# A chain of four layers on one core: the first batch in plain fp32, with filler products on TensorE between its steps

## The chip, the cores and the metric

The program runs on one core of a Trainium2 chip. The metric is the time of one execution in microseconds (us), the median of several runs. The engines are TensorE (PE in the profile, its weight loads PEld), VectorE (DVE), ScalarE (ACT), GpSimd (POOL) and SyncE (SP), whose queue issues most of the DMA transfers. Each engine works through its own list of instructions in order.

## The reference

Sixteen batches of a 256 x 256 matrix pass through four layers, each added to its input. Cut to what matters:

```python
# layer 0, per batch; ema(b, tau): h = alpha * h + b along the sequence
ctx = ema(x, tau_ctx)
gated = x * sigmoid(concat(x, ctx) @ Wg.T + bg)
mod = 0.5 + sigmoid(gelu(x @ Wn1.T + bn1) @ Wn2.T + bn2)      # 16 columns, one per decay
temporal = sum_d blend_w[d] * ema(gated * mod[..., d], tau[d])  # 16 decays
gate = sigmoid(temporal @ Wtemp.T + btemp)
soma = gelu(x @ Wsoma.T + bsoma)
x = x + layernorm((soma * gate) @ Wout.T) * gamma + beta
# layer 1: masked softmax over the sequence
scores = tanh(x @ W1 + b1) @ v
x = x + softmax(where(mask[type_b], scores, -1e30)) @ x / count
# layer 2: 8 experts and a shared one, all used by every batch (gates as factors)
x = x + sum_e c[b, e] * (silu(x @ Wg[e]) * (x @ Wu[e])) @ Wd[e]   # 9 experts of 256 x 1024
# layer 3: gelu MLP whose last 64 output columns use an expert chosen per batch
x = x + concat(h @ W2 + b2, h @ We[idx_b] + be[idx_b]),  h = gelu(x @ W1 + b1)
```

## The kernel before

*Products.* fp32 data are split into a high part that is rounded to fp32r, and a low part, the rest: `rnd` (L88 and L90) makes the first, `low` (L95) the second. `mm3` (L101 to L103) then makes three fp32r products in the place of one: high by high, high by low, low by high.

*Small weights.* Those of layers 0 and 1 (N1, G, SO, TE, OU, W1 for Wn1, Wg, Wsoma, Wtemp, Wout and layer 1's W1) are loaded by `load_small` (L127) into tiles that belong to other work and split by `split_small` into wh and wl.

*Layers 0 and 1.* Two generators hand them out in steps: `traces(b)` (21 steps, or 13 for batch 0) up to temporal, `pooled(b)` (10 steps) for the rest. Names to follow in the trace: ph, hg, hs are the hidden layer of mod; pm, md, ms its output; pg and ga the gate; pb and mod the factor of one decay, bt the scan's input, tr its output, ta their sum, t its copy; pso and sm the soma. Then pt and g (gate), s, po (Wout), st, mv, rs (layernorm), x1, ptr (transpose), u and x1T, pa, th, ths (tanh), psc (scores), sc (softmax), ppt and q (transpose), pp, acc. Batch 0 (`fast`) has forms of its own: its 16 decays' sums are made on TensorE by a product with the identity (L344), its factors come from TensorE and ScalarE instead of by a transfer (mdd to mod), and its products go to two PSUM banks.

*Layers 2 and 3.* Expert weights come in 72 chunks of 384 KB, which `load_chunk` loads into one of two raw tiles and splits into one of ten ring tiles (L88, then L95 on VectorE or GpSimd). A unit (`l2_unit`) is the work of two chunks for one batch (256 columns), or of one chunk for a pair of batches (512 columns). Batch 0 rides alone for five experts, that is 20 units; then batch 1 boards and the two go on together; batches 2 and 3 board at expert pass 9 and so on. The second time a split chunk is seen, it is stored and then read back already split.

*Order.* The planner hands out steps of later batches between units; `FRONT` is the number of steps of batch 1's `traces` that are given out together with batch 0's `pooled`. A scheduler then fixes the list of each engine from priorities, with `issue_after` as an extra order for it. PSUM and SBUF tiles rotate in pools, so a tile waits for the last reader of the one before.

## Time and profile before

| what | value |
|---|---|
| runs | 2854.42, 2855.34, 2858.27 us, median 2855.34 |
| the profiled execution's own time | 2854.52 us |
| its span, first to last instruction | 2852.3 us |
| busy: TensorE, VectorE, GpSimd, ScalarE | 2781.6, 1442.2, 1295.4, 1239.2 us |
| mean granted TensorE clock | 0.993 |
| bytes moved | 371.24 MB |

The span leaves out 2.2 us around the instructions. The busy time of TensorE counts a product from its issue to a modelled end, so products that follow each other overlap, and a full TensorE is not one at its peak: what it does is read from how far the starts lie apart. In the rows below, the first number is the start or the stretch, and what stands in brackets is the idle time before an instruction and what ended it. Names are those of the tiles; `out<-in` gives them with partitions x elements.

### The profile page before, as it was taken

Reading aid. Unit: us, or ns where it says so; the run is one execution under the profiler, and the core shown is the slowest. Engines: PE = TensorE matmul, PEld = TensorE weight load, DVE = VectorE, ACT = ScalarE, POOL = GpSimd, SP = SyncE. Lnnn points to the kernel's source line nnn. Section 1 sums busy time; section 2 is a strip of 40 time slices with the busy share of each in tenths; the row PEclk is TensorE's granted clock in tenths of the full one; section 3 lists DMA queues with packets and bytes.
Section 4 is the critical chain, followed back from the end, with each engine's and each line's share of the span. In section 5 each row is a group of like instructions: output and inputs, shape, how many; then the busy total and the mean of one; then the engine's idle time right before and its main releaser. Section 6 shows DMA issues by size and latency. Waiting matters only on the chain. (4 is left out here: it accounts for less than half of the span.)

```text
span 2852.3 us, 36958 instructions
## 1 busy us (share of the span) xinstructions
PE 2781.6 (98%) x13632; PEld 2339.8 (82%) x13632; DVE 1442.2 (51%) x2661; ACT 1239.2 (43%) x2054; POOL 1295.4 (45%) x984
## 2 busy tenths in 40 slices
PE   6889889999999999999999999999999999999999
PEld 4887778888888888888888888888888888888887
DVE  7978866665665454444544445444444542222222
ACT  5565544456444533435334443344433453233433
POOL 4755544544645453543534445344454443333333
PEclk8999999999999999999999999999999999999999
DMA  3444546547443532323433143332523242222552
GB/s 106 132 144 137 162 149 217 176 144 244 149 159 120 172 123 100 118 80 92 173 105 125 40 167 117 107 118 66 181 100 110 93 159 98 89 89 76 189 196 86
DMA packets 114694, 371.24 MB, mean 130 GB/s; under 512 B 12642, under 2 KB 30930, under 8 KB 114514
## 3 DMA queue, kind: packets, MB, share of 16 engines
q1 hardware_dynamic: 113650, 368.74, 39.0%
q8 instruction: 108, 1.77, 0.3%
q14 instruction: 72, 0.59, 0.1%
q10 hardware_dynamic: 864, 0.14, 0.0%
HBM read 304.62 MB, written 64.21 MB: 129 GB/s over the span
## 5 line engine op out<-in xcount | busy, mean ns | idle before, releaser
L95 POOL TENSOR_TENSOR hh<-h,hh 128x512 fp32r<-128x512 f32 x640 | 848.4, 1326 | 1327.1 <-ACT hh L88 1307.4
L608 DVE TENSOR_TENSOR h<-h,pu 128x512 f32<-128x512 f32 x576 | 393.9, 684 | 939.6 <-PE pu L103 818.1
L88 ACT ACTIVATE hh<-h 128x512 fp32r<-128x512 f32 x640 | 403.5, 631 | 932.6 <-DVE h L608 912.4
L101 PE MATMUL pg<-x,w_e 128*128 128x512 f32 (+1 forms) x1232 | 467.3, 379 | 12.7 <-ACT x L88 5.4
L607 ACT ACTIVATE h<-pg 128x512 f32<-128x512 f32 x576 | 342.9, 595 | 306.6 <-PE pg L103 228.5
L101 PE MATMUL pu<-x,w_e 128*128 128x512 f32 (+1 forms) x1232 | 465.4, 378 | 6.5 <-ACT h L607 3.7
L103 PE MATMUL pg<-x,w_e 128*128 128x512 f32 (+1 forms) x1232 | 465.7, 378 | 4.2 <-DVE w_e L95 3.4
L102 PE MATMUL y<-hh,w_e 128*128 128x512 f32 (+1 forms) x1232 | 464.4, 377 | 3.2 <-POOL hh L95 3.2
L102 PE MATMUL pg<-x,w_e 128*128 128x512 f32 (+1 forms) x1232 | 465.3, 378 | 0.0
L103 PE MATMUL pu<-x,w_e 128*128 128x512 f32 (+1 forms) x1232 | 463.8, 376 | 0.0
L102 PE MATMUL pu<-x,w_e 128*128 128x512 f32 (+1 forms) x1232 | 463.6, 376 | 0.0
L103 PE MATMUL y<-hh,w_e 128*128 128x512 f32 (+1 forms) x1232 | 463.5, 377 | 0.0
L101 PE MATMUL y<-hh,w_e 128*128 128x512 f32 (+1 forms) x1232 | 415.6, 377 | 1.0 <-DVE acc L655 0.8
L367 POOL TENSOR_TENSOR ta<-ta,tr 128x512 f32<-128x512 f32 x225 | 308.4, 1371 | 67.6 <-DVE tr L363 53.9
L363 DVE TENSOR_TENSOR_SCAN tr<-decay,bt 128x256 f32<-128x256 f32 x450 | 285.1, 672 | 0.0
L101 PEld LDWEIGHTS pg<-x,w_e 128*128 128x128 f32 x1232 | 232.5, 189 | 56.4 <-ACT w_e L88 6.4
L101 PEld LDWEIGHTS pu<-x,w_e 128*128 128x128 f32 x1232 | 232.1, 188 | 50.5 <-ACT h L607 5.8
L103 PEld LDWEIGHTS pg<-x,w_e 128*128 128x128 f32 x1232 | 232.7, 189 | 47.8 <-DVE w_e L95 5.2
L102 PEld LDWEIGHTS y<-hh,w_e 128*128 128x128 f32 x1232 | 233.0, 189 | 47.0 <-POOL hh L95 5.5
L101 PEld LDWEIGHTS y<-hh,w_e 128*128 128x128 f32 x1232 | 231.5, 189 | 44.8 <-ACT hh L88 1.3
L103 PEld LDWEIGHTS y<-hh,w_e 128*128 128x128 f32 x1232 | 233.0, 189 | 41.7
L103 PEld LDWEIGHTS pu<-x,w_e 128*128 128x128 f32 x1232 | 232.3, 189 | 41.9
(294 smaller groups left out, 3267.5 us busy)
## 6 DMA issues: line engine op xcount, KB each, us to landing
w_e<-keep_e SPq DMA_DIRECT2D x216, 768.0 KB, 4.4
raw_e<-in_wexp_dram SPq DMA_DIRECT2D x144, 384.0 KB, 4.5
keep_e<-w_e SPq DMA_DIRECT2D x72, 768.0 KB, 4.2
mod<-mdd SPq DMA_DIRECT2D x120, 256.0 KB, 3.5
w_f<-keep_f SPq DMA_DIRECT2D x56, 384.0 KB, 3.6
raw_c<-in_comb_dram SPq DMA_DIRECT2D x32, 260.0 KB, 2.8
xr<-in_xT_dram SPq DMA_DIRECT2D x16, 256.0 KB, 3.1
xt<-in_x_dram SPq DMA_DIRECT2D x16, 256.0 KB, 2.7
```

What stands on the lines that cost most here:

```text
L88: last_of["ca"] = A.activation(out_, in_, AF.Copy)
L95: i = (V if e == "v" else G).tensor_tensor(out_, in_, h.bitcast(F32), ALU.subtract)
L101: PE.matmul(o, wh, xh, start=start, stop=False, **kw)
L102: PE.matmul(o, wh, xl, start=False, stop=False, **kw)
L103: last_of["pe"] = PE.matmul(o, wl, xh, start=False, stop=stop, **kw)
L363: V.tensor_tensor_scan(tr[:, c], decay[:, d : d + 1].to_broadcast([P, S]), bt[:, c], 0.0, ALU.mult, ALU.add)
L367: G.tensor_tensor(tacc, tacc, tr, ALU.add)
L607: A.activation(h, ps_g, AF.Silu)
L608: last_of["h"] = V.tensor_tensor(h, h, ps_u, ALU.mult)
```

## The change

Batch 0 gets two generators of its own, `first_traces` and `first_pooled`, and `traces` and `pooled` keep only the form of the others. In them every product but that of ms with sel (pb) is one fp32 product instead of three fp32r products, taken straight from the raw weights (`small`) and from unsplit data; only ms and the input of the experts (x2) are still split. The raw small weights stay in two tiles of the pools xs and accp. Their splits, which the other batches need, are handed to ScalarE and GpSimd: N1 and G behind batch 0's `first_traces`, SO, TE, OU and W1 with four decays of batch 1 (the scheduler may place them earlier). `warm(n)` puts out n fp32 products of the identity with itself, 128 columns each, into a PSUM tile that nobody reads: 10 at the start and 5, 7, 2 and 10 behind the products pt, po, pa and psc. Constants that batch 0's first steps don't need come later (`later_constants`, `coefs`), the loads of pti, sgt and gat go from ScalarE's DMA queue to SyncE's, sm of batch 0 lies in PSUM, and batch 1 gets 3 steps in place of 4 beside batch 0 (`FRONT0`).

```diff
+FRONT0 = 3
...
-    small = {}
-
-    def load_small(c0, c1, tag):
-        raw = l0.tile([P, 512], F32, tag=tag, name=f"raw_{c0}", bufs=L0_BUFS.get(tag, 1))
-        nc.sync.dma_start(raw[:, : c1 - c0], wsmall[:, c0:c1])
-        small[c0] = raw[:, : c1 - c0]
-
-    def split_small(c0, e):
-        raw = small.pop(c0)
-        c1 = c0 + raw.shape[1]
-        rnd("a", wh[:, c0:c1], raw)
-        low(e, wl[:, c0:c1], raw, wh[:, c0:c1])
+
+    raw_a = xs.tile([P, 2048], F32, tag="x2", name="small_a")
+    raw_b = accp.tile([P, 1024], F32, tag="acc", name="small_b")
+
+    def small(off, n):
+        if O_TE <= off < O_W1:
+            return raw_b[:, off - O_TE : off - O_TE + n]
+        c = off if off < O_TE else off - O_W1 + O_TE
+        return raw_a[:, c : c + n]
+
+    def load_small(c0, c1):
+        nc.sync.dma_start(small(c0, c1 - c0), wsmall[:, c0:c1])
+
+    def split_small(c0, n, e):
+        rnd("a", wh[:, c0 : c0 + n], small(c0, n))
+        low(e, wl[:, c0 : c0 + n], small(c0, n), wh[:, c0 : c0 + n])
...
-    load_small(O_N1, O_N1 + 256, "bt")
+    load_small(O_N1, O_N1 + 256)
     bl = const([P, 2, ND], F32, "bl", blend)
-    load_small(O_G, O_G + 512, "tr")
     vec = const([P, V_COLS], F32, "vec", vecs)
-    pti = const([P, NB], I32, "pti", ptype.partition_broadcast(P))
-    sgt = const([P, NB], F32, "sgt", sgate.partition_broadcast(P))
-    gat = const([P, NB, NE], F32, "gat", gates.partition_broadcast(P))
-    load_small(O_G + 512, O_G + 1024, "tr")
-    load_small(O_SO, O_SO + 512, "xo")
-    load_small(O_TE, O_TE + 512, "sc")
-    load_small(O_OU, O_OU + 512, "x1")
-    load_small(O_W1, O_W1 + 256, "mb")
+    load_small(O_G, O_G + 512)
+    load_small(O_G + 512, O_G + 1024)
+    pti = const([P, NB], I32, "pti", ptype.partition_broadcast(P), nc.sync)
+    load_small(O_SO, O_SO + 512)
+    load_small(O_TE, O_TE + 512)
+    load_small(O_OU, O_OU + 512)
+    load_small(O_W1, O_W1 + 256)
     xt_tiles = {0: load_xt(0)}
     gam = const([P, S], F32, "gam", gamma.partition_broadcast(P), nc.sync)
     bet = const([P, S], F32, "bet", beta.partition_broadcast(P), nc.sync)
     eix = const([1, NB], I32, "eix", eidx, nc.sync)
+    sgt = const([P, NB], F32, "sgt", sgate.partition_broadcast(P), nc.sync)
+    gat = const([P, NB, NE], F32, "gat", gates.partition_broadcast(P), nc.sync)
...
+    def later_constants():
...
+    def coefs():
+
+        V.tensor_copy(coef[:, :, NE], sgt)
+        V.tensor_scalar(sgt, sgt, -1.0, 1.0, ALU.mult, ALU.add)
+        V.tensor_tensor(coef[:, :, 0:NE], gat, sgt.unsqueeze(2).to_broadcast([P, NB, NE]), ALU.mult)
...
+    rest = {1: (O_SO, 512), 6: (O_TE, 512), 9: (O_OU, 512), 12: (O_W1, 256)}
+
+    def traces(b):
...
-        if fast:
-            split_small(O_N1, "v")
...
-        if fast:
-            with tc.issue_after(last_of["cx"].ins):
-                split_small(O_G, "v")
-                split_small(O_G + 512, "v")
-
-                V.tensor_copy(coef[:, :, NE], sgt)
-                V.tensor_scalar(sgt, sgt, -1.0, 1.0, ALU.mult, ALU.add)
-                V.tensor_tensor(coef[:, :, 0:NE], gat, sgt.unsqueeze(2).to_broadcast([P, NB, NE]), ALU.mult)
...
+            if b == 1 and d in rest:
+                split_small(*rest[d], "g")
...
+    def two(name):
+
+        return [ps_gu.tile([P, 512], F32, tag="gu", name=f"{name}{t}")[:, :S] for t in "gu"]
+
+    def evict(c, o, i):
+
+        if c == 0:
+            last_of["ca"] = A.activation(o, i, AF.Copy)
+        else:
+            last_of["cv"] = V.tensor_copy(o, i)
+
+    idle = ps_y.tile([P, 512], F32, tag="y1", name="idle")
+
+    def warm(n, after=None):
+
+        with tc.issue_after(after.ins) if after is not None else nullcontext():
+            for _ in range(n):
+                PE.matmul(idle[:, :P], ident, ident, start=True, stop=True)
+
+    def first_traces():
+        xr = xin_tiles.pop(0)
+        warm(10)
+        cx = ft("ta", "ctx0")
+        for c in range(2):
+            last_of["cx"] = V.tensor_tensor_scan(
+                cx[:, c], decay[:, ND : ND + 1].to_broadcast([P, S]), xr[:, c], 0.0, ALU.mult, ALU.add
+            )
+        yield
+        ph = ps_l.tile([P, 512], F32, tag="ps", name="ph0")
+        for k in range(2):
+            PE.matmul(ph[:, :S], small(O_N1 + k * P, P), xr[:, k], start=k == 0, stop=k == 1)
+        hg = l0.tile([P, S], F32, tag="hg", name="hg0")
+        A.activation(hg, ph[:, :S], AF.Gelu, bias=vec[:, V_BN1 : V_BN1 + 1])
+        pg = two("pg0")
+
+        def gates_of(ks):
+            for m in range(2):
+                for k in ks:
+                    i = xr[:, k] if k < 2 else cx[:, k - 2]
+                    PE.matmul(pg[m], small(O_G + k * S + m * P, P), i, start=k == 0, stop=k == 3)
+
+        gates_of((0, 1))
+        yield
+        pm = ps_l.tile([P, 512], F32, tag="ps", name="pm0")
+        last_of["pm"] = PE.matmul(pm[:48, :S], vec[0:64, V_WN2 : V_WN2 + 48], hg[0:64], start=True, stop=True)
+        md = l0.tile([48, S], F32, tag="md", name="md0")
+        A.activation(md, pm[:48, :S], AF.Tanh, bias=hb[:48, V_BN2 : V_BN2 + 1], scale=0.5)
+        V.tensor_scalar(md, md, 0.5, 1.0, ALU.mult, ALU.add)
+        ms = l0.tile([48, S], F32R, tag="ths", name="ms0")
+        rnd("v", ms, md)
+        low("v", ms[32:], md[32:], ms[32:])
+        yield
+        ga = ft("ga", "ga0")
+        with tc.issue_after(last_of["pm"].ins):
+            gates_of((2, 3))
+        for m in range(2):
+            A.activation(ga[:, m], pg[m], AF.Tanh, bias=hb[:, V_BG + m : V_BG + m + 1], scale=0.5)
+        for c in range(2):
+            V.scalar_tensor_tensor(ga[:, c], ga[:, c], 1.0, xr[:, c], ALU.add, ALU.mult)
+        yield
+        sm = ps_a.tile([P, 2, S], F32, tag="ga", name="sm0")
+
+        tacc = ps_y.tile([P, 2, S], F32, tag="y0", name="ta0")
+        for d in range(ND):
+            if d % 2 == 0:
+                pb = ps_gu.tile([P, 2, S], F32, tag="gu", name=f"pb0_{d}")
+                for i in range(2):
+                    last_of["pb"] = PE.matmul(
+                        pb[:, i], sel[:, d + i : d + i + 1].to_broadcast([48, P]), ms, start=True, stop=True
+                    )
+            mod = l0.tile([P, 2, S], F32, tag="mod", name=f"mod0_{d}", bufs=2)
+            for c in range(2):
+                last_of["a"] = A.activation(mod[:, c], pb[:, d % 2], AF.Copy, scale=bl[:, c, d : d + 1])
+            bt = ft("bt", f"bt0_{d}", 3)
+            e = "g" if d else "v"
+            last_of[e] = (V if e == "v" else G).tensor_tensor(bt, ga, mod, ALU.mult)
+            tr = ft("tr", f"tr0_{d}", 3)
+            for c in range(2):
+                last_of["tr"] = V.tensor_tensor_scan(
+                    tr[:, c], decay[:, d : d + 1].to_broadcast([P, S]), bt[:, c], 0.0, ALU.mult, ALU.add
+                )
+            PE.matmul(tacc, ident, tr, start=d == 0, stop=d == ND - 1)
+            if d == 5:
+                pso = ps_l.tile([P, 2, S], F32, tag="ps", name="pso0")
+                with tc.issue_after(last_of["pb"].ins):
+                    for m in range(2):
+                        for k in range(2):
+                            w = small(O_SO + k * S + m * P, P)
+                            PE.matmul(pso[:, m], w, xr[:, k], start=k == 0, stop=k == 1)
+                for m in range(2):
+                    A.activation(sm[:, m], pso[:, m], AF.Gelu, bias=vec[:, V_BSO + m : V_BSO + m + 1])
+            if d % 2:
+                yield
+        t = ft("bt", "t0", 3)
+        for c in range(2):
+            evict(c, t[:, c], tacc[:, c])
+        xt = xt_tiles.pop(0)
+        with tc.issue_after(last_of["g"].ins):
+            last_of["g"] = G.tensor_tensor(xt, xt, bet.unsqueeze(1).to_broadcast([P, 2, S]), ALU.add)
+        held[0] = xt, sm, t
+        yield
+
+    def first_pooled():
+        xt, sm, tt = held.pop(0)
+        mb = l0.tile([P, 2, S], F32, tag="mb", name="mb0")
+        kreg = nc.sync.value_load(kind_i[0:1, 0:1], min_val=0, max_val=2)
+        nc.sync.dma_start(mb, masks[bass.ds(kreg, 1)].rearrange("o p c s -> (o p) c s"))
+        pt = two("pt0")
+        sg = ft("g2", "g20")
+        for m in range(2):
+            for k in range(2):
+                i = PE.matmul(pt[m], small(O_TE + k * S + m * P, P), tt[:, k], start=k == 0, stop=k == 1)
+        warm(5, i)
+        for m in range(2):
+            last_of["ca"] = A.activation(sg[:, m], pt[m], AF.Tanh, bias=hb[:, V_BTE + m : V_BTE + m + 1], scale=0.5)
+        yield
+        for c in range(2):
+            last_of["cv"] = V.scalar_tensor_tensor(sg[:, c], sg[:, c], 1.0, sm[:, c], ALU.add, ALU.mult)
+        yield
+
+        po = two("po0")
+        st = l0.tile([P, 2, 6], F32, tag="st", name="st0")
+        mv = l0.tile([P, 2, 2], F32, tag="mv", name="mv0")
+        rs = l0.tile([P, 2], F32, tag="rs", name="rs0")
+        for k in range(2):
+            for t in range(2):
+                w = small(O_OU + k * S, S)
+                i = PE.matmul(po[t], sg[:, k, t * P : (t + 1) * P], w, start=k == 0, stop=k == 1)
+        warm(7, i)
+        x1 = ft("x1", "x10")
+        for t in range(2):
+            V.bn_stats(st[:, t], po[t])
+            V.bn_aggr(mv[:, t], st[:, t])
+        V.tensor_scalar(rs, mv[:, :, 1], 4e-5, None, ALU.add)
+        G.tensor_tensor(rs, rs, mhalf, ALU.pow)
+        for t in range(2):
+            V.scalar_tensor_tensor(po[t], po[t], mv[:, t, 0:1], gam, ALU.subtract, ALU.mult)
+        yield
+        for t in range(2):
+            last_of["cv"] = V.scalar_tensor_tensor(
+                x1[:, t], po[t], rs[:, t : t + 1], xt[:, t], ALU.mult, ALU.add
+            )
+        yield
+
+        ptr = two("ptr0")
+        for c in range(2):
+            for t in range(2):
+                PE.transpose(ptr[c][:, t * P : (t + 1) * P], x1[:, t, c * P : (c + 1) * P], ident)
+        x1T = ft("xo", "x1T0")
+        for c in range(2):
+            evict(c, x1T[:, c], ptr[c])
+        yield
+        pa = ps_l.tile([P, 512], F32, tag="ps", name="pa0")
+        for k in range(2):
+            i = PE.matmul(pa[:, :S], small(O_W1 + k * P, P), x1T[:, k], start=k == 0, stop=k == 1)
+        warm(2, i)
+        ta = l0.tile([P, S], F32, tag="th", name="th0")
+        last_of["ca"] = A.activation(ta, pa[:, :S], AF.Tanh, bias=vec[:, V_B1 : V_B1 + 1])
+        yield
+        psc = ps_l.tile([P, 512], F32, tag="ps", name="psc0")
+        i = PE.matmul(psc[:, :S], vec[0:64, V_V : V_V + 1].to_broadcast([64, P]), ta[0:64], start=True, stop=True)
+        warm(10, i)
+
+        sc = ft("sc", "sc0")
+        mx = l0.tile([P, 2], F32, tag="mx", name="mx0")
+        sums = l0.tile([P, 2], F32, tag="sums", name="sums0")
+        for j in range(2):
+            V.tensor_tensor_reduce(
+                sc[:, j], psc[:, :S], mb[:, j], -1.0, 3e38, ALU.add, ALU.min, mx[:, j : j + 1]
+            )
+            last_of["ca"] = A.activation(
+                sc[:, j], sc[:, j], AF.Exp, bias=mx[:, j : j + 1], scale=-1.0, accum_out=sums[:, j : j + 1]
+            )
+        yield
+        for j in range(2):
+            js = slice(j, j + 1)
+            V.tensor_tensor(sums[:, js], sums[:, js], cntb[:, 0, js], ALU.mult)
+            V.reciprocal(sums[:, js], sums[:, js])
+            last_of["cv"] = V.tensor_scalar(sc[:, j], sc[:, j], sums[:, js], None, ALU.mult)
+        yield
+        ppt = two("ppt0")
+        for l in range(2):
+            for j in range(2):
+                PE.transpose(ppt[l][:, j * P : (j + 1) * P], sc[:, j, l * P : (l + 1) * P], ident)
+        q = ft("bt", "q0", 3)
+        for l in range(2):
+            evict(l, q[:, l], ppt[l])
+        yield
+        pp = two("pp0")
+        for l in range(2):
+            for m in range(2):
+                PE.matmul(pp[m], x1[:, l, m * P : (m + 1) * P], q[:, l], start=l == 0, stop=l == 1)
+        for m in range(2):
+            V.tensor_tensor(acc_of(0)[:, m], x1T[:, m], pp[m], ALU.add)
+        for m in range(2):
+            split_x2(0, slice(m, m + 1), "a")
...
-            alone[len(phases) - 1] = FRONT
+            front = FRONT if b else FRONT0
+            alone[len(phases) - 1] = front
             phases.append([(traces, b + 1)])
-            ready.append(count + FRONT)
+            ready.append(count + front)
...
-                    gens[f, b] = f(b, b == 0)
+                    gens[f, b] = f(b) if b else first[f]()
...
+    first = {traces: first_traces, pooled: first_pooled}
...
+        if n_steps[0] == 4:
+            with tc.issue_after(last_of["cx"].ins):
+                later_constants()
+    with tc.issue_after(last_of["a"].ins), tc.issue_after(last_of["g"].ins), tc.issue_after(last_of["tr"].ins):
+        for off, n in ((O_N1, 256), (O_G, 512), (O_G + 512, 512)):
+            split_small(off, n, "g")
...
+        coefs()
         prefetch(RING - n)
```

## The prediction

> **What bounds the kernel now.** I read the page first, then busy time by stretch, the timeline of each engine in the first 75 us, and last the waits of the DMA queue.
>
> ```profile
> span 2852.3 us, 36958 instructions
> ...
> PE   6889889999999999999999999999999999999999
> ...
> DVE  7978866665665454444544445444444542222222
> ```
>
> ```profile
> 50.00:60.00 10.00, 5.04 (x22) 3.75 (x21) 7.02 (x15) 4.44 (x10) 2.51 (x3) 0.67 0.25 74
> 60.00:70.00 10.00, 6.47 (x32) 5.66 (x30) 5.18 (x15) 4.44 (x10) 1.50 (x1) 0.59 0.58 189
> ...
> 450.00:500.00 50.00, 50.00 (x292) 44.22 (x291) 29.93 (x45) 26.19 (x43) 19.06 (x15) 1.00 0.55 185
> ```
>
> A slice of the page is 71.3 us. From the seventh on TensorE is at 9, and from 400 us on the stretches show it busy without a gap: whatever is gained or lost before 400 us arrives unchanged at the end. In the first slice nothing is full: it is one chain, batch 0 alone, and its end is the first expert product. The timeline of TensorE, with the gap before an instruction in brackets:
>
> ```profile
> 29.74 1.98 PE L344 MATMUL ta<-tr,ident 128*128 128x512 f32 x4
> ...
> 34.43 8.63 PE L344 MATMUL ta<-tr,ident 128*128 128x512 f32 x16
> 43.53 0.39 PE L101 MATMUL pt0g<-t,wh 128*128 128x256 f32 x1 [0.47 <-ACT t L88]
> ...
> 48.05 0.58 PE L427 MATMUL po0g<-wh,s 128*128 128x256 f32 x1 [2.44 <-ACT s L88]
> 48.43 0.42 PE L428 MATMUL po0g<-wl,s 128*128 128x256 f32 x1
> ...
> 72.81 0.38 PE L101 MATMUL pg<-x,w_e 128*128 128x256 f32 x1 [0.73 <-ACT x L88]
> ```
>
> The other engines' lines that time this chain (ScalarE, GpSimd, VectorE):
>
> ```profile
> 12.05 0.63 ACT L88 ACTIVATE wh<-raw 128x512 fp32r<-128x512 f32 x1 [2.43 <-DMA raw<-in_wsmall_dram]
> ```
>
> ```profile
> 22.14 18.44 POOL L338 TENSOR_TENSOR bt<-ga,mod 128x512 f32<-128x512 f32 x15 [4.97 <-ACT mod L335]
> ```
>
> ```profile
> 60.30 1.35 DVE L90 CAST ths<-th 128x256 fp32r<-128x256 f32 x1
> ```
>
> So batch 0 has three parts: 22.1 us until GpSimd's first bt; 18.4 us of 15 bt at 1.23 us, GpSimd's pace; then 32.2 us (40.58 to 72.81) of short steps that wait for each other. Behind it, from 72.8 to 190.2 us, batch 0's 20 expert units run alone. What bounds that stage is in the DMA queue's waits of 72 to 192 us (total, times, longest):
>
> ```profile
> SPq L536 <- DVE w_e L95: 43.5, 19, 4.9
> SPq L536 <- POOL w_e L95: 25.1, 11, 3.0
> ```
>
> The load of the next expert chunk waits for a raw buffer (there are two) that VectorE or GpSimd has not split yet. Chunk 6 is rounded at 73.0 us and chunk 40 at 188.4: 3.4 us each, where a chunk's 18 products of 256 columns at 0.118 us are 2.1. VectorE is full from 80 to 120.
>
> **The change, part by part.**
>
> *Front (0 to 22.1).* N1, G, x and ctx are no longer split for batch 0: 3 weight splits on VectorE (1.6 us) and x's two operations (1.1) go, and the products need only the loads. But in the changed program ScalarE, which works in order, has the rounding of SO and TE ahead of the gelu of ph, and that of OU and W1 ahead of md. TE landed at 12.05; with sgt and gat moved behind it I take 11.5. Then: round TE 0.63, table load 1.28, gelu 0.48: 13.9. pm (one fp32 product, cold): 14.8. Rounding of OU and W1 (1.0) fits beside pm. md 0.46, then md, ms, low 0.97: 16.4. The four gate products on ctx stand behind pm: cold 0.85 each (3.43 us is two 512-column sums, so 1.71 each, half for 256) gives 18.2, warm (1.98 for two, so 0.50 each) 16.9. I take cold, since the clock was last warmed before 7 us. pb, ga1, mod_0, mod_1 (0.43, 0.47, 2 x 0.84): first bt at 20.5 against 22.14. The fp32 soma (4 products, 2 to 3.4 us) now sits before the sums, and its gelu holds mod_3 up by about 0.4. Gain 1.2; bounds -0.5 (TE not earlier, all cold) and 3.9 (warm, TE 1 us earlier).
>
> pti, sgt and gat move from ScalarE's DMA queue to SP's: three issues of 0.45 us at most, so the first two chunk loads (12.44) go out 1.3 us later; they are not used before 38.9. The 20 small operations that move behind ctx's scan (0.17 us each, 3.4 us) run while VectorE waits for md. GpSimd gets SO, TE, OU, W1 in front (4.5 us, ending near 17) under the same cover; without it they would delay the first bt one for one.
>
> *Scan loop.* Unchanged: 15 bt of 1.23 us.
>
> *Tail, counted from the last bt (40.58 before).* The last sum is done at 2.5. GpSimd has, in the new order, xt 1.28, N1 0.65, G 2 x 1.28, two chunks 3.6, x of batch 1 1.25: it is through at 9.4, so raw buffer 0 is free at 6.3 (before: 1.8), and chunk 2 lands at 9.4. Evict t, 3.4. pt, four products of 0.50: 4.95, with g's tanh at 5.5. No rounding of g: two STT at about 1.0 beside GpSimd (the row of before: 1.02) to 7.0; po starts at 6.05 and ends at 8.05. Two scans of batch 1 hold VectorE to 8.3; statistics, mean and rs 1.6; pow 0.70, 10.7; x1 to 11.65 (before 14.9). Then VectorE has chunk 2, c and hs of batch 1 ahead of x1T's second half: 14.1. pa, tanh: 15.25 (before 19.0). psc directly, 15.8; scores, exp, scale as before 2.5, plus 0.3 for the table load that used to be hidden by ths: 18.6 (before 25.1: ths took 1.35 and 0.42, and the 24 gate products of batch 1 stood ahead of ppt until 68.7). ppt 19.1; ScalarE rounds chunks 4 and 5 and does md ahead of q: 20.0. pp, four products: 22.05; acc, rounding of x: first expert product at 22.6. Before: 32.2. Gain 9.6, and the first expert product stands at 62.0 instead of 72.8.
>
> *Products that nobody reads.* 34 of 128 columns in fp32: 0.25 us each warm, 0.43 cold, a quarter of the sum's rows. The ten at the start end near 5.7, when x has just landed. The later ones (5, 7, 2, 10: 1.25, 1.75, 0.5, 2.5 us warm) end before their successor is ready by the tail above, but for the five, 0.15 late. [...] The trace: pt's products follow each other in 0.12 us, and po's, after a gap of only 2.44 us, in 0.21: the clock was already down (the stretches show a granted clock of 0.67 and 0.59). [...] By the trace they are what keeps pt to pp at 0.50. If they fail, 11 products at 0.85 cost 3.9 us, and the idle ones, twice as long, push po, ptr and ppt by some 3. I go by the trace and take them as working.
>
> *What comes back in the expert stage.* FRONT0 = 3 moves batch 1's 24 gate products behind unit 0 (2.8 us of a stage where TensorE waits anyway) and its two tanh behind chunks 8 and 9 on ScalarE, hence ahead of unit 1's silu. Chunks 6 and 7 land only 0 to 1 us after the first expert product (before they lay ready), coef's three operations (1.7) run there too. By this, unit 1's silu comes some 9 us after the first expert product (before 5.1), batch 1's first bt 10 (before 4.4). VectorE's long full stretch so starts with 4 us less done. Full cover (the chunk pipe alone sets the pace) costs 0, none costs 5; with VectorE full to 128 us I take 3. At the boarding of batch 1 (190 us) its last products pp now stand one unit and a third later; the pair then waited 2.5 us for a chunk in any case, so I add nothing.
>
> **Sum.** 1.2 + 9.6 - 3 = 7.8 us off the profiled execution's 2854.5 us: 2846.7. The median of the runs is 0.8 above that execution: 2847.5. A difference under 0.2% (5.7 us) counts as none below.
>
> **Rivals.** *Half eaten (no change):* the clock falls between the steps. Gain 10.8 - 6.9 for cold products - 3 = 0.9, so 2854.4. For it: 0.59 and 0.67 in these stretches; against: five of the gaps are filled. The same figure comes out if GpSimd's 4.5 us of new splits hold chunk 2, and ScalarE and VectorE stand behind it, longer than I count. *Batch 1 late at its boarding (slower):* the lag grows with each chunk, and the pair that boards at unit 20 finds batch 1 unscored. The price is seen where batch 3 boards: from its scores' product at 381.7 until 398.8 us TensorE has only that chain, 17 us. Then -10.8 + 3 + 17: 2864. It decides once batch 1's lag exceeds some 8 us, two units, at unit 17. Against it: only one step more of batch 1 has to be placed in these 20 units. *All of it kept:* warm at the front and no lag, 3.9 + 9.6: 2841. *The change does nothing:* excluded for the tail, since splits vanish from its path.
>
> **How the numbers follow.** Main case 0.57 (2847.5, own range 2842 to 2853; about 7 in 10 of it lies under 2849.6, which is 5.7 below the median), all kept 0.2 (2841, 2837 to 2845), no change 0.09 (2850 to 2858), late 0.14 (2861 to 2870). Faster: 0.57 x 0.7 + 0.2 = 0.6; slower by over 5.7 us: the late case, 0.14; the rest, 0.17 + 0.09, is 0.26. The range is 2839 to 2858: the late case lies outside, and a quarter of the case that keeps all, 0.19 together. The bounds of the front (-0.5 to 3.9), of the lag (0 to 5) and some 2 us for the new order of instructions up to 400 us lie within it.
>
> **What would show it.** First bt near 20.5 and ScalarE's gelu near 13.9, behind the rounding of TE; po's fp32 products 0.5 us apart, not 0.85; chunk 2 landing after GpSimd's splits; first expert product near 61 to 63; batch 1's first bt ten us later; the first pair product near 182 (190.2 before), and the same distance at 400 us and at the end. Wrong: a first expert product later than 66, a gap of several us before the first pair, or an end that moved by something else than the first pair did.

## The result, and the profile after

| what | before | after |
|---|---|---|
| median of 8 runs each, us | 2855.33 | 2845.68 |
| lowest and highest run | 2852.84, 2858.44 | 2843.57, 2849.85 |
| the profiled execution: own time, span | 2854.52, 2852.3 | 2843.57, 2841.8 |
| GpSimd's first bt | 22.14 | 16.65 |
| GpSimd's last bt ends | 40.58 | 35.17 |
| first expert product | 72.81 | 56.73 |
| first pair product | 190.21 | 185.55 |

The ratio of the runs is 0.9967, 95% interval [0.9956, 0.9978]: 9.65 us off the median, more than the 0.2% (5.7 us) that counts as a change here. The forecast was 7.8 us off (2847.5). The sum comes out close, but its three terms do not: the front gave 5.5 us (forecast 1.2), the tail 10.7 (9.6), and 5.6 came back (3).

First the page of the changed kernel, span and busy tenths of TensorE and VectorE, 71 us a slice:

```profile
span 2841.8 us, 37013 instructions
...
PE   8889989999999999999999999999999999999998
...
DVE  7878766665665364544545445444444542222222
```

The picture is the old one: TensorE is full from the seventh slice on but for the last, and what changed most lies in the first (6 tenths before, 8 after). Busy time by stretch (TensorE, its weight loads, VectorE, ScalarE, GpSimd, then granted clock, DMA share, GB/s):

```profile
50.00:60.00 10.00, 8.77 (x62) 7.58 (x62) 6.66 (x22) 6.68 (x14) 2.48 (x2) 1.00 0.55 148
60.00:70.00 10.00, 10.00 (x85) 9.95 (x85) 5.23 (x9) 6.31 (x10) 3.84 (x3) 1.00 0.60 181
...
450.00:500.00 50.00, 50.00 (x310) 45.07 (x309) 28.91 (x45) 26.32 (x42) 17.07 (x13) 1.00 0.60 206
```

The clock stays at 1.00 where it was 0.67 and 0.59. The front, on ScalarE:

```profile
8.02 0.63 ACT L89 ACTIVATE wh<-small_a 128x512 fp32r<-128x512 f32 x1 [1.82 <-DMA small_a<-in_wsmall_dram]
8.70 0.63 ACT L89 ACTIVATE wh<-small_b 128x512 fp32r<-128x512 f32 x1
...
10.64 0.47 ACT L499 ACTIVATE hg<-ph,vec 128x256 f32<-128x256 f32 x1
```

and GpSimd's scan loop:

```profile
16.65 18.52 POOL L542 TENSOR_TENSOR bt<-ga,mod 128x512 f32<-128x512 f32 x15 [2.84 <-ACT mod L539]
```

TE (small_b) is rounded right behind SO, at 8.70 instead of 12.05, without a wait of its own, and the gelu follows at 10.64. The loop lasts as long as before. The tail, on TensorE:

```profile
38.13 0.70 PE L578 MATMUL pt0g<-t,small_b 128*128 128x256 f32 x2 [0.47 <-ACT t L474]
38.66 0.59 PE L578 MATMUL pt0u<-t,small_b 128*128 128x256 f32 x2
...
39.96 1.28 PE L484 MATMUL idle<-ident 128*128 128x128 f32 x10
41.07 0.60 PE L594 MATMUL po0g<-small_b,g 128*128 128x256 f32 x2
41.51 0.59 PE L594 MATMUL po0u<-small_b,g 128*128 128x256 f32 x2
...
50.33 2.50 PE L484 MATMUL idle<-ident 128*128 128x128 f32 x20
...
56.73 0.39 PE L102 MATMUL pg<-x,w_e 128*128 128x256 f32 x1 [0.53 <-ACT x L89]
```

An fp32 product of 256 columns stands as two records and takes 0.43 us warm (granted clock 1.00); the three fp32r products that it replaces take 3 x 0.118 at that clock. So at the same clock the products themselves got slower. What left the path is roundings, low parts and their waits: po starts 2.94 us after pt (before 4.52).

Here is where the time came back. In the single units batch 0 stood 9 to 18 us ahead of the kernel before (the silu of unit 16 at 154.67 against 172.54), but the first pair product is only 4.7 us ahead. That is not yet the end of it: the kernel before then stands still (TensorE busy 7.47 of the 10 us from 190 to 200, the changed kernel 10.00), and at the second pair unit's silu the lead is 9.6 us (192.45 against 202.00). It is 8.7 at unit 41, and constant at 10.5 from about 450 us on. Two lines of the kernel before:

```profile
172.54 0.60 ACT L607 ACTIVATE h<-pg 128x512 f32<-128x512 f32 x1
...
190.21 0.39 PE L101 MATMUL pg<-x,w_e 128*128 128x512 f32 x1
```

In the changed kernel, on ScalarE ahead of unit 17, and on TensorE ahead of the first pair:

```profile
164.16 0.84 ACT L89 ACTIVATE w_e<-raw_e 128x768 fp32r<-128x768 f32 x1 [4.16 <-DMA raw_e<-in_wexp_dram]
...
166.32 0.60 ACT L758 ACTIVATE h<-pg 128x512 f32<-128x512 f32 x1
```

```profile
183.35 0.38 PE L102 MATMUL pso<-x,wh 128*128 128x256 f32 x1 [2.01 <-DVE acc L461]
...
185.55 0.63 PE L102 MATMUL pg<-x,w_e 128*128 128x512 f32 x1
```

ScalarE stands 4.16 us before a chunk that has not landed, with unit 17's silu behind it; and the soma of batch 2 waits in TensorE's list for batch 1's acc.

### The profile page after: what moved, and what is told of

Same layout as the page of the kernel before. It is cut to its first block, busy times and chain, and to the rows that moved or that the text cites. A ratio compares the mean times of both kernels' runs of the same rounds, so it can differ in the third digit from the quotient of the medians.

```text
span 2841.8 us, 37013 instructions
## 1 busy us (share of the span) xinstructions
PE 2785.5 (98%) x13672; PEld 2343.8 (82%) x13672; DVE 1426.0 (50%) x2646; ACT 1235.8 (43%) x2043; POOL 1295.6 (46%) x986
## 3 DMA queue, kind: packets, MB, share of 16 engines
q8 instruction: 108, 1.77, 0.3%
```

## The experiments

Each kernel ran on a chip beside the kernel before (medians there 2854.46 to 2855.68). Where two of the medians are compared, up to 1.2 us can be the chip, and the intervals of the ratios reach 2.6 to 4 us to either side. "Given back" is the lead at the first expert product less the lead of the span, both against the profiled kernel before; it belongs to one execution.

| kernel | first bt | first expert product | first pair | span | given back | median and range of runs |
|---|---|---|---|---|---|---|
| after | 16.65 | 56.73 | 185.55 | 2841.8 | 5.6 | 2845.68 (2843.57 to 2849.85) |
| no idle products | 16.38 | 59.98 | 185.73 | 2840.1 | 0.6 | 2841.07 (2840.80 to 2841.95) |
| idle at the start only | 16.89 | 59.25 | 185.42 | 2839.6 | 0.9 | 2841.37 (2839.94 to 2843.39) |
| queues back | 20.98 | 61.23 | 193.44 | 2851.9 | 11.2 | 2851.67 (2848.89 to 2855.99) |
| FRONT0 = 4 | 16.61 | 63.85 | 183.96 | 2845.7 | 2.4 | 2847.93 (2843.49 to 2855.00) |
| fp32 alone | 18.29 | 64.06 | 183.40 | 2846.0 | 2.5 | 2849.36 (2847.20 to 2853.65) |

**1. No idle products.**

```diff
-            for _ in range(n):
+            for _ in range(0):
                 PE.matmul(idle[:, :P], ident, ident, start=True, stop=True)
```

> The changed kernel without its 34 products that nobody reads; all other instructions and nearly their whole order are as they were. Theory (the idle products keep the clock up, as po's spacing of 0.21 us after a gap of 2.44 us in the kernel before lets expect): the granted clock between 36 and 57 us falls to about 0.6 to 0.8, the fp32 products of pt, po, pa and pp stand some 0.85 us apart instead of 0.43, so that the first expert product comes at 59 to 63 us instead of 56.73; at the front GpSimd's first bt comes at 17 to 19 us instead of 16.65; in all 2849 to 2852 us. [...]

Measured: ratio 0.9953 [0.9940, 0.9967]. Each of its five runs is faster than each of the changed kernel's eight. Its stretches and TensorE's tail:

```profile
40.00:50.00 10.00, 6.58 (x27) 4.45 (x25) 8.33 (x18) 4.57 (x9) 6.15 (x6) 0.82 0.46 143
50.00:60.00 10.00, 7.59 (x19) 3.87 (x17) 5.06 (x17) 5.36 (x11) 1.36 (x1) 0.50 0.47 149
```

```profile
45.21 0.38 PE L103 MATMUL ph<-x,wh 128*128 128x256 f32 x1 [1.53 <-POOL x L96]
...
46.55 0.47 PE L614 MATMUL ptr0g<-ident,x 128*128 128x128 f32 x1 [0.47 <-DVE x L606]
...
48.48 2.08 PE L621 MATMUL pa<-x1T,small_a 128*128 128x256 f32 x4 [0.82 <-ACT x1T L474]
...
59.98 0.46 PE L102 MATMUL pg<-x,w_e 128*128 128x256 f32 x1
```

The theory holds for the clock and the first expert product: 0.50 in place of 1.00, pa's two products in 2.08 us where the changed kernel's took 1.48, and the first unit 3.25 us later. It fails for the time: without the idle products the kernel is 4.6 us faster by the medians, and 3.7 when each is set against the kernel before on its own chip. The lead of 3.25 us is gone at the first pair product (185.73 against 185.55), though the lists behind the tail are the same. By 400 us this execution is 2.0 us ahead. Two waits of ScalarE for a chunk show where, first in the changed kernel and then without idle products:

```profile
297.25 0.84 ACT L89 ACTIVATE w_e<-raw_e 128x768 fp32r<-128x768 f32 x1 [5.30 <-DMA raw_e<-in_wexp_dram]
```

```profile
165.09 0.84 ACT L89 ACTIVATE w_e<-raw_e 128x768 fp32r<-128x768 f32 x1 [2.97 <-DMA raw_e<-in_wexp_dram]
...
294.50 0.85 ACT L89 ACTIVATE w_e<-raw_e 128x768 fp32r<-128x768 f32 x1 [3.52 <-DMA raw_e<-in_wexp_dram]
```

At 165 the wait is 2.97 us instead of 4.16. The later chunk was rounded 5.6 us after its issue (291.69) in the changed kernel, 3.8 (290.72) here: the same transfer in the same list. What makes the difference is taken up behind experiments 10 and 11.

**2. The loads of pti, sgt and gat back on ScalarE's queue.**

```diff
+    pti = const([P, NB], I32, "pti", ptype.partition_broadcast(P))
+    sgt = const([P, NB], F32, "sgt", sgate.partition_broadcast(P))
+    gat = const([P, NB, NE], F32, "gat", gates.partition_broadcast(P))
     load_small(O_G + 512, O_G + 1024)
-    pti = const([P, NB], I32, "pti", ptype.partition_broadcast(P), nc.sync)
...
-    sgt = const([P, NB], F32, "sgt", sgate.partition_broadcast(P), nc.sync)
-    gat = const([P, NB, NE], F32, "gat", gates.partition_broadcast(P), nc.sync)
```

> pti, sgt and gat again on ScalarE's DMA queue, ahead of the small weights, as in the kernel before; TensorE's and GpSimd's lists are unchanged. Theory (the front's 5.5 us are mostly these loads: they held up TE, whose rounding stands ahead of the gelu of ph on ScalarE): TE is rounded at 11 to 12 us instead of 8.70, the gelu of ph comes near 13.5 instead of 10.64, GpSimd's first bt at 19 to 20 us, and the time is 2848 to 2849. Rival (the front's gain is the absence of the splits and the warm clock): first bt within 0.7 us of 16.65, and the time within 1.5 us of 2845.7.

Measured: ratio 0.9989 [0.9980, 0.9998]. ScalarE and GpSimd:

```profile
11.31 0.63 ACT L89 ACTIVATE wh<-small_b 128x512 fp32r<-128x512 f32 x1 [2.70 <-DMA small_b<-in_wsmall_dram]
11.95 1.28 ACT L499 ACT_TABLE_LOAD   x1
13.25 0.47 ACT L499 ACTIVATE hg<-ph,vec 128x256 f32<-128x256 f32 x1
```

```profile
20.98 2.49 POOL L542 TENSOR_TENSOR bt<-ga,mod 128x512 f32<-128x512 f32 x2 [4.66 <-ACT mod L539]
```

The theory holds at the front in kind: TE is again awaited, 2.6 us later, the gelu too, and the first bt is 4.3 us later, outside the 19 to 20 us that were expected. The further 1.7 us go with the clock: between 10 and 20 us it is 0.66 (1.00 in the changed kernel), and the eight records of the gate products on ctx, behind a gap of 5.03 us, take 3.8 us instead of 2.0. The time is 6.0 us worse, more than either theory gave: in this execution 11.2 us come back in the expert stage.

**3. FRONT0 = 4.** (`-FRONT0 = 3`, `+FRONT0 = 4`)

> FRONT0 = 4 in place of 3: batch 1's 24 gate products and their two tanh go back between batch 0's steps. Theory of the prediction (what the expert stage gives back is batch 1's lag at its start): the first expert product comes 2 to 3 us later than 56.73, the give-back shrinks from 5 us to 2 to 3, and the time is 2844 to 2847. Rival (the lag at the start is made good by unit 8 anyway, and the give-back arises at the boarding of batch 1): the first expert product is 2 to 3 us later, and the give-back is as it was or larger: 2848 to 2850.

Measured: ratio 0.9977 [0.9968, 0.9986]. The first expert product is 7.1 us later, not 2 to 3. TensorE shows why:

```profile
53.28 4.63 PE L484 MATMUL idle<-ident 128*128 128x128 f32 x20
57.57 0.56 PE L102 MATMUL pg<-x,wh 128*128 128x256 f32 x1
...
63.85 0.39 PE L102 MATMUL pg<-x,w_e 128*128 128x256 f32 x1 [0.80 <-ACT x L89]
```

Here psc waited 2.05 us and took 1.22 us instead of 0.70, as in experiment 1 at a granted clock of 0.50, and the ten idle products behind it took 4.63 us instead of 2.50, with the gate products of batch 1 and ppt in line behind them. The give-back does shrink to 2.4, the size that the prediction's theory asks for (but see experiments 1 and 5, which have the lag and give back less): single units take 120.1 us from first expert product to first pair with FRONT0 = 4, and 128.8 in the changed kernel. The two nearly cancel; the time lies on the border of the two ranges, 2.25 us above the changed kernel.

**4. A third raw buffer.**

```diff
-    raws = ctx.enter_context(tc.tile_pool(name="raws", bufs=2))
+    raws = ctx.enter_context(tc.tile_pool(name="raws", bufs=3))
...
-        hg = l0.tile([P, S], F32, tag="hg", name=f"hg{b}")
+        hg = l0.tile([P, S], F32, tag="th", name=f"hg{b}")
...
-        hs = l0.tile([P, S], F32R, tag="hs", name=f"hs{b}")
+        hs = l0.tile([P, S], F32R, tag="ths", name=f"hs{b}")
```

> A third raw buffer for the expert chunks (the room comes from letting hg share th's tile and hs share ths's). Theory (from 57 to 185 us the pipe of load, rounding, split sets the pace, because a load waits for one of two raw buffers: 69 us of such waits stood in the stage): the stage of 20 single units gets 5 to 15 us shorter, and since the time after 400 us only shifts, 2832 to 2841. Rival (VectorE's work for batch 1 and ScalarE's place in order set the stage, not the buffers): the queue's waits shrink, TensorE's waits don't, and the time stays within 2 us of 2845.7.

Measured: ratio 1.0000 [0.9991, 1.0009], 8.7 us worse than the changed kernel: outside both. The units did get faster (silu of unit 19 at 168.46 instead of 179.76), and then TensorE stood before batch 1:

```profile
181.26 1.17 PE L445 MATMUL ppt<-ident,sc 128*128 128x128 f32 x4 [6.68 <-DVE sc L437]
...
194.63 0.38 PE L102 MATMUL pso<-x,wh 128*128 128x256 f32 x1 [2.76 <-DVE acc L461]
...
196.98 0.63 PE L102 MATMUL pg<-x,w_e 128*128 128x512 f32 x1
```

So the two buffers set the pace of the units, but the end of the stage is batch 1's own chain, and it is later here (its scores are scaled at 180.85 instead of 160.58). That the faster chunks alone delay it is not shown, for hg and th share a tile as well: this is the prediction's rival of a late batch 1, met where it was not looked for.

**5. Idle products at the start only.** (`range(n if after is None else 0)` in warm)

> The changed kernel with the ten idle products at the start alone; the 24 behind pt, po, pa and psc are left out. Theory (the first expert product comes later without them, but the stage behind it ends no later, because batch 1's own chain sets the boarding): first bt as in the changed kernel at 16.65, clock below 0.9 between 40 and 57 us, first expert product at 58.5 to 59.5 instead of 56.73, and the time 2840 to 2842. Rival (what made the kernel without any idle products faster is its front, where ScalarE's order differs: the gelu of ph ahead of the roundings of SO and TE): the time is 2844 to 2847.

Measured: ratio 0.9952 [0.9939, 0.9966]. All points of the theory hold: clock 0.92 from 40 to 50 us and 0.57 from 50 to 60, first expert product 59.25, first pair 185.42. So the 24 products in the tail cost the 4 us, whatever they cost it by; the ten at the start make no difference that these runs tell.

**6. and 7. Two parts alone, on the kernel before.** In 6 the loads of sgt and gat go to SyncE's queue and coef's operations behind batch 0; in 7 the 34 idle products are added at the same places.

```diff
-    sgt = const([P, NB], F32, "sgt", sgate.partition_broadcast(P))
-    gat = const([P, NB, NE], F32, "gat", gates.partition_broadcast(P))
...
     eix = const([1, NB], I32, "eix", eidx, nc.sync)
+    sgt = const([P, NB], F32, "sgt", sgate.partition_broadcast(P), nc.sync)
+    gat = const([P, NB, NE], F32, "gat", gates.partition_broadcast(P), nc.sync)
```

> The kernel before with one part of the change: the loads of sgt and gat go to SyncE's queue behind eix, and coef's three operations behind batch 0. Theory (these two loads held up the small weights, which ScalarE waits for): TE is rounded at 9 to 10 us instead of 12.05, GpSimd's first bt comes 2 to 3 us earlier than 22.14, all behind it moves with it since no list changes in the expert stage, and the time is 2851 to 2853. Rival (VectorE's splits set the front, not the loads): first bt within 0.7 us of 22.14, time 2853.8 to 2855.5.

> The kernel before with the other separate part: the 34 idle products at the same places (10 at the start, 5, 7, 2 and 10 behind pt, po, pa and psc), all splits kept. Theory (the clock is up in the tail, and fp32r products gain by it): granted clock 1.00 instead of 0.67 and 0.59 between 50 and 70 us, po's products 0.12 us apart instead of 0.21, the 24 gate products of batch 1 the same, first expert product 2 to 3.5 us earlier than 72.81, time 2851 to 2853. Rival (idle products cost what they win, as the changed kernel without them suggests): first expert product within 1 us of 72.81, time 2854 to 2856.

Measured: 6 gives 2853.54 us, ratio 0.9995 [0.9986, 1.0004]; TE is rounded at 10.09 instead of 12.05, but the first bt comes only 0.8 us earlier (21.35), nearer to the rival: with splits in the front the loads are not what is waited for. 7 gives 2855.01, ratio 0.9998 [0.9989, 1.0007]; the first expert product gains 0.3 us, the clock between 50 and 70 us rises to 0.78 and 0.71 only. Its rival holds.

**8. No idle products, mask later.** In `pooled(b)` the two lines that load mb stand ahead of ptr.

> The changed kernel without idle products, and in pooled(b) of the later batches the load of the 256 KB mask moved from the start to just ahead of the transposes ptr. At the start it is issued as soon as the batch before has read its mask, that is at 160.6 us, among two factor loads and two chunk loads, and the chunk issued at 160.0 took until 165.1 to be rounded. Theory (transfers that meet there hold up the chunk, ScalarE and so the silu of unit 17): this chunk is rounded 0.7 to 2 us earlier, the first pair product comes 0.5 to 2 us earlier than 185.73, and the time is 2839 to 2840.5. Rival (the boarding hangs on VectorE's list, not on the transfer): 2840.5 to 2841.8.

Measured: 2840.19 us (2838.42 to 2840.70), ratio 0.9945 [0.9932, 0.9959], the fastest kernel of all: 14.5 us off the kernel before beside it, 0.9 under experiment 1. But the edit hardly took hold: the first five masks stand in SyncE's list where they stood (at 159.84 the one that was meant), and up to 400 us only reads of registers changed places there. The theory was not tried, and the 0.9 us are not the mask's: they lie before 400 us, where the two kernels' lists agree. So much two such kernels may differ, and experiments 1, 5 and 8 are best read as one result: without idle products in the tail the kernel beats both that it began with.

**9. The tail's idle products moved into the scan loop.** The 24 of the tail are left out, and behind pso stand 24 of one column.

```diff
+                with tc.issue_after(i.ins):
+                    for _ in range(24):
+                        PE.matmul(idle[:, :1], ident, ident[:, :1], start=True, stop=True)
```

> The changed kernel with the ten idle products at the start; the 24 others stand not in the tail but in the scan loop behind pso, one column each. TensorE's list is thus from the first expert unit on as long as in the changed kernel, and the first expert product as late as with the front's ten alone (59.25). Code theory (TensorE's list of instructions is itself fetched by transfers of their own, whose places depend on how many instructions stand ahead; in the changed kernel such a fetch fell at 154 us and at 294 us, just where two chunk loads landed late; at 164 and elsewhere without the 24): the fetch comes near 156 us again, what is lost between units 16 and 41 too, and the time is 2844 to 2848. Rival (only the start counts: the stage gives back a lead in any case, and takes nothing from a later start): 2840 to 2842.

Measured: 2859.62 us, ratio 1.0015 [1.0006, 1.0025], first expert product at 72.02 instead of 59.25, so that its time answers nothing. Its stretches, and TensorE's list at the end of the one-column products:

```profile
20.00:30.00 10.00, 10.00 (x34) 7.03 (x34) 5.14 (x9) 1.73 (x5) 3.73 (x4) 0.58 0.07 24
30.00:40.00 10.00, 10.00 (x22) 5.18 (x21) 3.76 (x6) 4.75 (x12) 5.75 (x5) 0.50 0.00 1
```

```profile
30.95 1.28 PE L558 MATMUL idle<-ident 128*128 128x1 f32 x6
...
33.09 2.07 PE L548 MATMUL ta<-tr,ident 128*128 128x512 f32 x2
```

TensorE's list ran without a gap, and the clock fell to 0.50 all the same. It stayed there until about 42 us, though the last one-column product is over at 32.2, so these products alone don't explain it. The sums of the decays (fp32, 512 columns, 0.86 us warm) then took twice as long, more than GpSimd's 1.23 us for a bt, and TensorE set the pace of the loop. From the first expert product on, though, this kernel has the changed kernel's lists and as many TensorE products ahead of them; that is used next.

**10. and 11. Wider idle products; the same with the mask later.**

```diff
+            for c in () if after is None else {5: (512,), 7: (448, 448), 2: (256,), 10: (512, 512, 256)}[n]:
+                PE.matmul(idle[:, :c], ident, raw_a[:, :c], start=True, stop=True)
```

> The changed kernel with the idle products of the tail wider and fewer: 1 of 512 columns, 2 of 448, 1 of 256 and 3 of 512, 512 and 256, in place of 5, 7, 2 and 10 of 128; as many columns, 17 instructions fewer, all other lists the same. Code theory: the first expert product stays within 0.5 us of 56.73, the fetch of TensorE's code moves from 154 to some 160 us, what is lost between units 16 and 41 shrinks, and the time is 2838.5 to 2842. Rival (a lead at the start of the stage is given back whatever the code): first expert product the same, time 2844.5 to 2847.

> The wide idle products, and the mask's load ahead of the transposes ptr. Theory: the two add up: 0.5 to 1.5 us below the kernel with the wide idle products alone, so 2837.5 to 2841. Rival (the mask's load only moved another transfer's place): within 0.5 us of it or above.

Measured: 2844.60 (ratio 0.9963 [0.9949, 0.9976]) and 2844.07 (0.9961 [0.9947, 0.9974]). The profiled execution of 10 has its first expert product at 61.89, not 56.73, with VectorE's, ScalarE's and GpSimd's lists unchanged: W1's weights landed later (ScalarE waited 1.58 us for them), the fp32 soma took 3.55 us instead of 1.99 (granted clock 0.83 between 10 and 20 us, 1.00 in the changed kernel), and the idle products behind psc took 4.11 us (0.66 between 50 and 60 us). That of 11, warm at these places, has 57.83. Both times miss the code theory's range. For the mask, kernel 11 tells no more than experiment 8.

The code theory had a third point, what is lost between units 16 and 41, and there the traces speak for it. The page of the changed kernel lists transfers of the kind "instruction" on a queue q8, 108 of 1.77 MB in all, 16 KB each; between two of them, from 154 to 294 us, lie 20.6 to 35.8 us and 110 to 137 of TensorE's products (127 in the mean of all 13672). A fetch, here and below, is such a transfer of q8; that it brings TensorE's code is the author's reading. Eight kernels have the same lists from the first expert product to 390 us; they differ in how many idle products TensorE has ahead of them, and with that in where a fetch falls (for each chunk, its issue, its rounding and the us between):

| kernel | idle products | fetch | one chunk | silu of unit 16 to that of unit 41 |
|---|---|---|---|---|
| after | 34 | 294.2 | 291.69, 297.25, 5.56 | 143.3 |
| queues back (2) | 34 | 301.4 | 299.06, 304.42, 5.36 | 144.3 |
| moved (9) | 34 | 308.4 | 305.86, 311.32, 5.46 | 142.6 |
| none (1) | 0 | 273.4, 307.4 | 290.72, 294.50, 3.78 | 138.2 |
| start only (5) | 10 | 268.6, 305.6 | 290.70, 294.43, 3.73 | 137.5 |
| none, mask later (8) | 0 | 272.4, 305.8 | 288.87, 292.62, 3.75 | 137.1 |
| wide (10) | 17 | 267.8, 306.2 | 294.49, 298.29, 3.80 | 138.8 |
| wide, mask later (11) | 17 | 264.4, 302.8 | 291.15, 294.90, 3.75 | 138.2 |

ScalarE's wait for this chunk in experiments 2, 9 and 10:

```profile
304.42 0.84 ACT L89 ACTIVATE w_e<-raw_e 128x768 fp32r<-128x768 f32 x1 [5.10 <-DMA raw_e<-in_wexp_dram]
```

```profile
311.32 0.84 ACT L89 ACTIVATE w_e<-raw_e 128x768 fp32r<-128x768 f32 x1 [5.21 <-DMA raw_e<-in_wexp_dram]
```

```profile
298.29 0.85 ACT L89 ACTIVATE w_e<-raw_e 128x768 fp32r<-128x768 f32 x1 [3.55 <-DMA raw_e<-in_wexp_dram]
```

The three kernels with 34 idle products, and only these, have a fetch between issue and rounding, and lose 4 to 7 us more in the stretch; this chunk alone is 1.7 us of that. It is not a lead that is taken back: experiments 2 and 10 reach the first expert product at 61.23 and 61.89 and unit 16 at 160.85 and 160.23, and unit 41 at 305.17 and 299.04; experiment 9 has hardly a lead (0.8 us). So the number of TensorE's instructions makes the loss, and the place of the fetch goes with it; how a fetch would hold a chunk up is not shown. Each kernel was traced once. The medians of 10 and 11 all the same stay some 3 us above those of 1 and 5; the late start of 10's trace is a part of that, the rest is open. With FRONT0 = 4, where the lists differ, 34 idle products cost nothing there (134.3 us in experiment 3, 135.0 with none in experiment 12).

**12. fp32 alone.** Experiments 1, 2 and 3 in one kernel.

> The changed kernel without idle products, with pti, sgt and gat again on ScalarE's queue and FRONT0 = 4: what is left of the change is batch 0's products in fp32 without splits (and the places of the small weights and constants). Theory (fp32 without splits carries the larger part by itself, the three other parts add up: 4.6 us gained by leaving out the idle products, 6.0 and 2.3 us lost by the queues and FRONT0): 2848 to 2851 us, that is 4 to 7 us under the kernel before; first expert product near 67 us. Rival (the fp32 products gain nothing unless TensorE is kept warm and the loads come early): 2853 to 2856.

Measured: 2849.36 us, ratio 0.9983 [0.9974, 0.9992], first expert product 64.06 (expected 67). The theory holds: fp32 without splits, with the new places of the small weights and constants, gives 5.3 us by itself. By the medians the parts add up to 2849.3; set against the kernel before on each chip they leave 3.4 us of gain instead of 5.3. So they add up to some 2 us, and the agreement to 0.1 is chance. By the single removals the queues bring 6.0 to 6.9 us, FRONT0 2.3 to 3.1, and the idle products take 3.7 to 4.6 back.

## Why the prediction came out

*Right in the sum, by terms that were off on both sides: that they cancelled to 2 us is luck.*

- **Front, 1.2 forecast, 5.5 measured: the mis-sized term is TE's landing.** The prediction let the queue's change bring it from 12.05 to 11.5. It came to 8.7. A second term is the clock: the gate products on ctx were taken cold and ran warm (granted 1.00), so that the first bt came 5.5 us behind the gelu's end, not 6.6. Experiment 2, where the loads stand as before, is a test of the rest of that working: rounding at 11.31, gelu at 13.25 (forecast 13.9), first bt at 20.98 (20.5). Three issues on another queue were booked as a delay of the chunks, and their absence from the front as half a microsecond. Experiment 6 shows the other half: the move (there of two of the three loads) is worth 0.8 us at the first bt while the splits stand in the path, 4.3 once they are gone.
- **Scan loop:** as forecast, 18.52 us.
- **Tail, 9.6 forecast, 10.7 measured.** GpSimd's row of splits and chunks came within 0.2 us (chunk 2 rounded 9.2 us behind the last bt, forecast 9.4). Two terms were too large: fp32 products at 0.50 each (0.43 measured) and the two STT at 1.0 each (0.85 for both).
- **Idle products: the step failed.** From po's 0.21 us behind a gap of 2.44 us in the kernel before, the prediction took it that the clock falls in the tail's gaps of 1 to 3 us. It did fall: without the idle products it was 0.50 from 50 to 60 us, with no gap over 1.53 us in the tail. But the price was wrong in size (6.9 forecast; 3.25 at the first expert product) and in sign at the end: the time is 4.6 us better without them. Two things are shown. When TensorE is cold at psc they are no filler but a block: 2.50 us warm, 4.11 and 4.63 cold (experiments 10 and 3), with ppt behind. And as instructions they have a price of their own, which the prediction put at nothing: with 34 of them the stretch from unit 16 to unit 41 takes 142.6 to 144.3 us, with 17 or fewer 137.1 to 138.8. In the two traces the changed kernel leads experiment 1 by 3.25 us at the first expert product and by 2.4 at unit 16, and is 2.8 behind at unit 41 and 1.7 at the end. The trace of the changed kernel is of its fastest execution; the rest of the 4.6 us between the medians lies in executions without a trace. Why the soma took 1.99 us in the changed kernel and 3.55 in experiment 10, with the same list ahead of it, is not shown; the gap ahead of pb, just before it, was 0.74 us in the one and 1.68 in the other.
- **Give-back, 3 forecast, 5.6 measured, and not for the reason given.** Batch 1's lag was there as worked out (unit 1's silu 10.4 us after the first expert product, forecast 9; batch 1's first bt 11.7, forecast 10). But it is not what came back: experiments 1 and 5 have the lag too and give back 0.6 and 0.9, and experiments 3 and 12 don't have it and give back 2.4 and 2.5. In the changed kernel the lead is largest at unit 16 (17.9 us) and falls to 8.7 by unit 41; in experiment 1 it falls from 15.5 to 11.4. The forecast's own signs say the same. The first pair product was to come near 182, with the same distance at 400 us and at the end; it came at 185.55, 4.7 us ahead, and the end moved by 10.5. An end that moves by something else than the first pair does stood there as a sign of being wrong, and for this term it was. What came back instead goes with the number of TensorE's instructions and the place of the fetches on q8 (table behind experiment 11). The prediction had no such term; by what step a fetch delays a chunk stays open.

Of the rivals, *half eaten* named a falling clock, which came where the idle products were left out, and at a smaller price than its 6.9 us (3.25); *late batch 1* did not come, and experiment 4 shows how near it lay: 11 us faster units, and the pair 11.4 us later than in the changed kernel.

## What to carry to other kernels

Filler work that keeps a clock up is in-order work: it must end ahead of its successor also at the low clock (here 2.50 us became 4.63), and its gain must be read at the end of the run, not at the next milestone. When a split or a copy leaves a chain, look again at loads that were hidden behind it; moving three small ones brought about as much as the arithmetic. Faster units don't shorten a stage that ends with another batch's chain (experiment 4). And instructions that were added or taken away moved the fetches on q8 (294.2 us with 34 idle products, 273.4 and 307.4 with none): here 4 to 7 us between two kernels went with that, so compare with one that has as many instructions.

## What the runs showed of the hardware

Unexpected were four things. A chunk of 384 KB was rounded 5.4 to 5.6 us after its issue in three kernels where a fetch on q8 fell in between, and 3.7 to 3.8 in five where none did (table behind experiment 11). The clock fell to 0.50 at about 21.6 us while TensorE's list ran without a gap, among products of one column and fp32 sums, and stayed there until about 42, ten us beyond the last of the narrow products (experiment 9); why is open. It fell after no gap longer than 1.53 us, in a stretch busy by 6.58 of 10 us (experiment 1). And an fp32 product of 256 columns took 0.43 us at a granted clock of 1.00 and 0.86 at 0.50 (experiment 1), against 0.35 at 1.00 for the three fp32r products that stand for it: splitting in three saved 0.08 us on TensorE, less than one rounding of 512 columns on ScalarE (0.63).
